# Turning the quantised activations of a two-product FFN by DMA instead of by TensorE

## The chip, the core and the metric

The kernel runs on one core of one Trainium2 chip. Its time is the device time of one launch in microseconds (us). Before the change it is 3245.24 us, the median of three runs (3242.97, 3245.24 and 3245.39).

## What is computed

A gated layer of a Flamingo-like model: cross-attention of 32 batches of 224 tokens (width 512, 16 heads of 32) to 750 context rows of width 384, and then a feed-forward network (FFN) whose two products take quantised activations and quantised weights. Cut to what matters here:

```python
def act_quant(x):                       # per row, to whole numbers of -128..127
    scale = 127.0 / clip(max(abs(x), axis=-1), 1e-5)
    return clip(round(x * scale), -128, 127) / scale
def weight_quant(w):                    # to -1, 0, 1, by the mean of |w|
    ...
def bitlinear(x, w, b):
    return act_quant(rmsnorm(x)) @ weight_quant(w).T + b

x = x + tanh(g_xattn) * cross_attention(layernorm(x), ctx)    # softmax over 750 rows
h = gelu(bitlinear(layernorm(x), w1, b1))                     # 512 -> 2048
x = x + tanh(g_ffn) * bitlinear(h, w2, b2)                    # 2048 -> 512
```

[...] Quantisation works along a row (a token's features), with the token in the partition. So each quantised activation has to be turned, from token x feature to feature x token, before its product can run. How that turning is done is what changes.

## The kernel before

**Two streams of work, woven into one order by hand.** The attention goes through 128 steps: 32 batches, and in each of them four groups of four heads. The loop of line 802 builds one step in six slots. In each slot it first emits a score block on TensorE: in the even slots `maxima` (line 276, tiles `sm`), whose rows VectorE reduces to maxima (`mx`); in the odd slots `weights` (line 333, tiles `se`), whose scores ScalarE exponentiates (`p`) and GpSimd adds up (`acc`). Both use the one PSUM buffer `s` of the pool `ps_s`. So TensorE can't begin a `weights` block before VectorE has read the `maxima` block ahead of it, nor the next `maxima` block before ScalarE has read the `weights` block. What TensorE does in between are the other products of the attention (`pk`, `pv`, `pq`, `po`, `pyt`) and the FFN.

**The FFN** takes 7168 tokens in 28 pairs of 128-row tiles (`ffn_units`, line 507). Per pair: load two tiles of the attention's result back from HBM into `xg` (`a_load`), statistics, centring on ScalarE (`xc`), row maximum, scales, multiplication onto the grid on GpSimd (`a_grid`), rounding to whole numbers in bf16 on ScalarE (`a_round`, tile `xq`, 128 x 1024 for the pair), turning (`a_turn`, line 564, tile `xT`). Then per tile: four products of 128 x 512 (`b_matmul`, `ph`) that VectorE scales into `h`, GELU and square on ScalarE, row maximum, scales, grid on GpSimd (`c_grid`), rounding on ScalarE (`c_round`, tile `hq`, 128 x 2048 bf16), turning in two halves (`c_turn`, line 623, tile `hT`), and two products of 128 x 256 (`c_matmul`, `po<-w2q,hT`), after which VectorE adds into `xg` and the SyncE queue stores the tile (`out`).

A turning by TensorE is one transpose for each 128 x 128 block: 8 for a pair's `xq`, 16 for a tile's `hq`, written to PSUM (`pxq`, `phq`) in bf16. ScalarE copies PSUM to SBUF, one copy of 128 x 1024 for each eight blocks.

**The planner.** `Ffn.fill` (line 727) is called in every slot. It puts in those FFN units that fit into the room left on TensorE, ScalarE and VectorE and that are `ready` (line 698). A unit is a tuple of name, lag, the unit that it follows, its cost on the three engines, and the function: `("turn", 1, "round", 0.6, 1.0, 0, a_turn)` is placed at least one slot after `round` and counts 0.6 us of TensorE and 1.0 us of ScalarE. The lag is counted in slots from the placing of the unit that it follows, not from its end. `before` in `ready` holds back units whose buffer isn't free yet. `xq`, `xT`, `hq` and `hT` have one buffer each (`fp`, `bufs=1`).

**Order on the engines.** Calls through `pe`, `dve`, `act` and `gp` (class `Ordered`, line 43) stay in program order on their engine. Calls of `nc.sync`, which issue all DMAs on the SyncE queue (SP), do not: a scheduler places them. [...] The profile gives nearly every instruction line 51, that of `Ordered`, so tiles tell them apart.

Of the kernel before, what the change touches and what calls it, by code (L numbers as in the profile page):

```python
# [9 lines left out]
BF16 = mybir.dt.bfloat16  # L10
# [14 lines left out]
def flamingo_gated_layer(  # L25
# [15 lines left out]
    nc = tc.nc  # L41
# [9 lines left out]
            return lambda *args, **kw: tc.keep_in_program_order(build(*args, **kw))  # L51

    pe, dve, act = Ordered(nc.tensor), Ordered(nc.vector), Ordered(nc.scalar)
    gp = Ordered(nc.gpsimd)
    P = 128
    B, S, D = x.shape
    CY, M = ctxT.shape[1], ctxT.shape[2]
# [25 lines left out]


    gates = const.tile([P, 2], F32, name="gates")
    nc.sync.dma_start(gates[:, 0:1], g_xattn.partition_broadcast(P))
    nc.sync.dma_start(gates[:, 1:2], g_ffn.partition_broadcast(P))
    tg = const.tile([P, 2], F32, name="tg")
    nc.scalar.activation(tg, gates, AF.Tanh)

    mask_u8 = const.tile([CP, B, NQ], U8, name="mask_u8")
    nc.sync.dma_start(mask_u8, maskT)
    qscale = const.tile([CP, B, NQ], F32, name="qscale")
    nc.vector.tensor_copy(qscale, mask_u8)
    nc.vector.tensor_scalar(qscale, qscale, DH ** -0.5, None, ALU.mult)
# [70 lines left out]

    def load_y(b):
        y_of[b] = yp.tile([P, NYC, M], F32, tag="y", name=f"y_{b}")  # L170
        nc.sync.dma_start(y_of[b], ctxT[b].rearrange("(c p) m -> p c m", p=P))

    def load_x(b):
        x_of[b] = xp.tile([CP, NQ, D], F32, tag="x", name=f"x_{b}")
        nc.sync.dma_start(x_of[b], x[b].rearrange("(t p) d -> p t d", p=CP))


    def q_units(b):
# [213 lines left out]
    def finish(b, g):  # L392

        oT = po_of.pop((b, g))
        pyt = ps_m.tile([P, 2, NQ, P], F32, tag="m", name=f"pyt_{b}_{g}")
        for a in range(2):
            for t in range(NQ):
                at = a * S + t * CP
                pe.transpose(pyt[:CP, a, t, :], oT[:, at : at + CP], ident)
        rd = smp.tile([CP, NQ, HG], F32, tag="rd", name=f"rd_{b}_{g}")  # L400
        dve.reciprocal(
            rd, pyt[:CP, 1].rearrange("p t (j d) -> p t j d", j=HG)[:, :, :, 0]
        )
        yo = smp.tile([CP, NQ, P], F32, tag="yo", name=f"yo_{b}_{g}")
        dve.tensor_tensor(
            yo.rearrange("p t (j d) -> p t j d", j=HG),
            pyt[:CP, 0].rearrange("p t (j d) -> p t j d", j=HG),
            rd.unsqueeze(3).to_broadcast([CP, NQ, HG, DH]),
            ALU.mult,
        )  # L410
        cols = slice(g * P, (g + 1) * P)
        gp.tensor_tensor(x_of[b][:, :, cols], x_of[b][:, :, cols], yo, ALU.add)
        if g == NG - 1:
            nc.sync.dma_start(
                x1_d[b * S : (b + 1) * S, :].rearrange("(t p) d -> p t d", p=CP), x_of[b]
            )


    def weight_units():
# [6 lines left out]
        def fetch(which, i, tag):  # L426
            wl = hp.tile([P, F // 2], F32, tag="h", name=f"{tag}_{which}_{i}")
            if which == 0:
                c, h = divmod(i, NW // NDC)
                n = F * NDC // NW  # L430
                nc.sync.dma_start(wl, w1T[c * P : (c + 1) * P, h * n : (h + 1) * n])
                held[tag, which, i] = wl, w1q[:, c, h * n : (h + 1) * n]
                return
            k = NFC // NW
            nc.sync.dma_start(
                wl.rearrange("p (k d) -> p k d", k=k),
                w2T[i * k * P : (i + 1) * k * P, :].rearrange("(k p) d -> p k d", p=P),
            )
            held[tag, which, i] = wl, w2q[:, i * k : (i + 1) * k, :].rearrange("p k d -> p (k d)")
# [47 lines left out]
    TG = 2  # L487
# [19 lines left out]
    def ffn_units(i):  # L507
# [5 lines left out]

        def a_load():
            s["xg"] = xgp.tile([P, TG, D], F32, tag="xg", name=f"xg_{i}")
            nc.sync.dma_start(s["xg"], x1_d[rows, :].rearrange("(t p) d -> p t d", p=P))

        def a_stats():
            st = smf.tile([P, TG, 6], F32, tag="st2", name=f"st2_{i}")
# [43 lines left out]

        def a_turn():
            s["xT"] = fp.tile([P, TG, NDC, P], BF16, tag="xT", name=f"xT_{i}")
            pt = ps_m.tile([P, TG, NDC, P], BF16, tag="m", name=f"pxq_{i}")
            for t in range(TG):
                for k in range(NDC):
                    pe.transpose(pt[:, t, k, :], s["xq"][:, t, k * P : (k + 1) * P], identb)
            act.copy(s["xT"], pt)  # L570

        def b_matmul(t, f):
            if f == 0:
# [45 lines left out]
        def c_round(t):  # L619
            s["hq", t] = fp.tile([P, F], BF16, tag="hq", name=f"hq_{i}_{t}")  # L620
            act.activation(s["hq", t], s.pop(("h", t)), AF.Identity, bias=magic)

        def c_turn(t, k8):
            if k8 == 0:
                s["hT", t] = fp.tile([P, NFC, P], BF16, tag="hT", name=f"hT_{i}_{t}")
            pt = ps_m.tile([P, 8, P], BF16, tag="m", name=f"phq_{i}_{t}_{k8}")
            for a in range(8):
                k = k8 * 8 + a
                pe.transpose(pt[:, a, :], s["hq", t][:, k * P : (k + 1) * P], identb)
            act.copy(s["hT", t][:, k8 * 8 : k8 * 8 + 8, :], pt)  # L630

        def c_matmul(t, half):
            cols = slice(half * D // 2, (half + 1) * D // 2)
            po = ps_m.tile([P, D // 2], F32, tag="m", name=f"po2_{i}_{t}_{half}")
            for k in range(NFC):
                pe.matmul(
                    po, s["hT", t][:, k, :], w2q[:, k, cols], start=(k == 0), stop=(k == NFC - 1)
                )
            o = s["xg"][:, t, cols]
            dve.scalar_tensor_tensor(o, po, s[f"qb{t}"][1], o, ALU.mult, ALU.add)  # L640
            if half:
                at = (i * TG + t) * P
                nc.sync.dma_start(out[at : at + P, :], s["xg"][:, t, :])

        first = [
            ("load", 0, None, 0, 0, 0, a_load),
# [6 lines left out]
            ("sa2", 1, "sa1", 0, 0, 0, lambda: a_scales(2)),  # L653
            ("grid", 0, "sa2", 0, 0, 0, a_grid),
            ("round", 2, "grid", 0, 1.1, 0, a_round),
            ("turn", 1, "round", 0.6, 1.0, 0, a_turn),
        ]
        parts = [first]
        for t in range(TG):
            part = []  # L660
            for f in range(4):
                part.append((
                    f"b{t}{f}", 0, f"b{t}0" if f else None, 0.9, 0, 0.75,
                    lambda t=t, f=f: b_matmul(t, f),
                ))
            part.append((f"gelu{t}", 1, f"b{t}3", 0, 1.9, 0, lambda t=t: b_gelu(t)))
            part.append((f"square{t}", 1, f"gelu{t}", 0, 1.9, 0, lambda t=t: b_square(t)))
            for a in range(2):
                part.append((f"hm{t}{a}", 1, f"gelu{t}", 0, 0, 1.2, lambda t=t, a=a: b_max(t, a)))
            part.append((f"sb{t}0", 1, f"square{t}", 0, 0, 0.2, lambda t=t: c_scales(t, 0)))  # L670
            part.append((f"sb{t}1", 2, f"sb{t}0", 0, 0, 0.2, lambda t=t: c_scales(t, 1)))
            part.append((f"sb{t}2", 1, f"sb{t}1", 0, 0, 0, lambda t=t: c_scales(t, 2)))
            part.append((f"cgrid{t}", 0, f"sb{t}2", 0, 0, 0, lambda t=t: c_grid(t)))
            part.append((f"cround{t}", 2, f"cgrid{t}", 0, 1.9, 0, lambda t=t: c_round(t)))
            for a in range(2):
                part.append((
                    f"cturn{t}{a}", 0 if a else 2, f"cturn{t}0" if a else f"cround{t}",
                    0.5, 1.0, 0, lambda t=t, a=a: c_turn(t, a),
                ))
            for a in range(2):  # L680
                part.append((
                    f"c{t}{a}", 0 if a else 1, f"c{t}0" if a else f"cturn{t}1",
                    1.8, 0, 0.4, lambda t=t, a=a: c_matmul(t, a),
                ))
            parts.append(part)
        return parts

    class Ffn:
# [9 lines left out]
        def ready(self, pair, unit):  # L698
# [12 lines left out]
            if name[-1].isdigit():  # L711
                t = int(name[len(name.rstrip("0123456789"))])
                (p1, t1), (ph, th) = (divmod(pair * TG + t - n, TG) for n in (1, HB))
                before = {
                    f"b{t}0": [(pair, "turn"), (ph, f"cround{th}"), (p1, f"b{t1}3")],
                    f"square{t}": [(p1, f"square{t1}")],
                    f"sb{t}0": [(pair, f"hm{t}0"), (pair, f"hm{t}1"), (p1, f"sb{t1}2")],
                    f"cround{t}": [(p1, f"cturn{t1}1")],
                    f"cturn{t}0": [(p1, f"c{t1}1")],
                }  # L720
            if name.startswith("square") and any(
                n == "norm" and (p, "round") not in self.at for p, n in self.at
# [44 lines left out]
    w_kv = wkvT.rearrange("(c p) e -> p c e", p=P)  # L767
    load_x(0)
    load_y(0)
    nc.sync.dma_start(wkv_sb[:, :, :D], w_kv[:, :, :D])  # L770
    nc.sync.dma_start(wq_sb, wqT.rearrange("(c p) e -> p c e", p=P))
    nc.sync.dma_start(wkv_sb[:, :, D:], w_kv[:, :, D:])
    load_y(1)
    load_x(1)
    nc.sync.dma_start(b1_sb, b1.partition_broadcast(P))
    nc.sync.dma_start(b2g, b2.partition_broadcast(P))
    norm, turns, qs = q_units(0)
    ks = k_units(0, 0) + k_units(0, 1)
    for unit in norm + ks[:2] + turns + qs[:1]:
# [131 lines left out]
```

## Time and profile before

One execution was profiled. It took 3241.06 us, and its profile spans 3239.3 us of them.

| | busy us | share of the span |
|---|---|---|
| TensorE matmuls (PE) | 3060.1 | 94% |
| TensorE weight loads (PEld) | 1976.6 | 61% |
| VectorE (DVE) | 1712.6 | 53% |
| ScalarE (ACT) | 1647.5 | 51% |
| GpSimd (POOL) | 2069.2 | 64% |
| DMA queue q1, of 16 engines | | 11.0% |

Busy time of TensorE counts a matmul from its start to its modelled end. Matmuls overlap, so the mean duration of a group is longer than what one of them takes from the next. The distance from one start to the next is the better price. The row of a group also tells how long its engine sat idle ahead of it and what ended that idle time ("<-").

### The profile page before, as it was taken

To read this page: it belongs to the slowest core of one execution; us is meant where nothing else is said; L and a number is where in the kernel's file an instruction comes from. 1 tells how busy PE (TensorE), PEld (TensorE's weight loads), DVE (VectorE), ACT (ScalarE), POOL (GpSimd) and SP (SyncE) were. 2 spreads that over 40 slices of the span, in tenths; PEclk is the share of its full clock that TensorE was granted. 3 is DMA by queue.
4 is the path that set the end of the run, shared out by engine and by line. 5 is a ranking of instruction groups with operands and counts; after the bars stand their busy time and mean duration, and the time that the engine had idled before them with its cause. 6 is when DMAs were issued, how large, how long until landed. Compare 5 with 4: busy or idle time off the path is not lost. (4 is left out here: it accounts for less than half of the span.)

```text
span 3239.3 us, 65769 instructions
## 1 busy us (share of the span) xinstructions
PE 3060.1 (94%) x28642; PEld 1976.6 (61%) x28642; DVE 1712.6 (53%) x2501; ACT 1647.5 (51%) x1803; POOL 2069.2 (64%) x3048
## 2 busy tenths in 40 slices
PE   7989999999999999999999999999999999999975
PEld 5655566666666666666666666666666666666643
DVE  4576555554465455555554554555555545545533
ACT  2333555555555455455555554555455455555554
POOL 2565667666666676667666666765676666667664
PEclk9999999999999999999999999999999999999988
DMA  3322111010101001101000111001100011110000
GB/s 134 103 75 65 33 40 40 16 39 26 40 30 36 26 25 33 37 32 40 20 29 30 40 36 39 27 16 40 40 30 26 26 33 37 36 40 20 4 20 29
DMA packets 52817, 120.51 MB, mean 37 GB/s; under 512 B 3888, under 2 KB 3888, under 8 KB 52400
## 3 DMA queue, kind: packets, MB, share of 16 engines
q1 hardware_dynamic: 52528, 116.32, 11.0%
q8 instruction: 223, 3.65, 0.5%
q14 instruction: 66, 0.54, 0.1%
HBM read 86.94 MB, written 29.36 MB: 36 GB/s over the span
## 5 line engine op out<-in xcount | busy, mean ns | idle before, releaser
L51 POOL TENSOR_TENSOR acc<-acc,p 125x896 f32<-125x896 f32 x512 | 1069.4, 2089 | 518.3 <-ACT p L51 497.4
L51 DVE TENSOR_REDUCE mx<-sm 112x4 f32<-112x2000 f32 (+1 forms) x384 | 860.9, 2242 | 986.6 <-PE sm L51 986.6
L51 ACT ACTIVATE p<-se 125x1792 f32<-125x1792 f32 x384 | 638.8, 1664 | 413.1 <-PE se L51 407.1
L51 PE MATMUL pk<-y,wkv_sb 128*128 128x375 f32 x1536 | 537.8, 486 | 15.8 <-DMA wkv_sb<-in_wkvT 12.1
L51 PE MATMUL sm<-kT,qT 32*112 32x500 f32 (+1 forms) x4096 | 426.8, 508 | 35.2 <-ACT p L51 34.7
L51 POOL TENSOR_TENSOR acc<-p 125x896 f32<-125x896 f32 x128 | 267.3, 2089 | 273.0 <-ACT p L51 272.9
L51 ACT COPY kT<-pk 128x375 f32<-128x375 f32 x256 | 120.8, 472 | 581.9 <-PE pk L51 581.3
L51 PEld LDWEIGHTS pk<-y,wkv_sb 128*128 128x128 f32 x1536 | 278.6, 190 | 172.2 <-issue 26.7
L51 PE MATMUL pv_None<-wkv_sb,y 128*125 128x256 f32 x1536 | 364.1, 387 | 0.0
L51 PE MATMUL se<-qT,kT 32*125 32x224 f32 x6144 | 362.7, 349 | 0.0
L51 PE MATMUL po<-p,v 125*32 125x224 f32 x6144 | 321.4, 358 | 0.1
L51 PEld LDWEIGHTS pv_None<-wkv_sb,y 128*125 128x125 f32 x1536 | 278.4, 187 | 69.8 <-issue 33.4
L51 PEld LDWEIGHTS se<-qT,kT 32*125 32x125 f32 x6144 | 297.8, 183 | 0.0
L51 DVE SCALAR_TENSOR_TENSOR h<-ph,qa_am,b_sb 128x512 f32<-128x512 f32 x224 | 163.5, 744 | 197.2 <-PE ph L51 196.1
L51 PEld LDWEIGHTS sm<-kT,qT 32*112 32x112 f32 x4096 | 159.2, 170 | 166.8 <-issue 94.4
L51 PEld LDWEIGHTS po<-p,v 125*32 125x32 f32 x6144 | 188.1, 111 | 115.1 <-issue 40.1
L51 PE MATMUL ph<-w1q,xT 128*128 128x512 fp8e4 x896 | 226.8, 385 | 26.2 <-ACT xT L51 24.0
L51 PE MATMUL po<-w2q,hT 128*128 128x256 fp8e4 x1792 | 221.3, 279 | 13.1 <-DVE xg L51 7.1
L51 PE MATMUL pq<-xnT,wq_sb 128*128 128x224 f32 x1024 | 218.2, 356 | 0.2 <-ACT xnT L51 0.2
L51 PE MATMUL se<-nT,ones 3*125 3x448 bf16 x1536 | 157.2, 396 | 54.2 <-DVE mx L51 45.4
L51 POOL TENSOR_TENSOR x<-x,yo 112x256 f32<-112x256 f32 x128 | 100.6, 786 | 165.3 <-DVE yo L51 135.4
L51 PEld LDWEIGHTS <-hT 128*128 128x128 bf16 x1792 | 174.5, 100 | 48.3 <-issue 17.9
(102 smaller groups left out, 3497.3 us busy)
## 6 DMA issues: line engine op xcount, KB each, us to landing
y<-in_ctxT SPq DMA_DIRECT2D x32, 1125.0 KB, 5.4
x<-in_x SPq DMA_DIRECT2D x32, 448.0 KB, 3.9
x_d<-x SPq DMA_DIRECT2D x32, 448.0 KB, 3.1
xg<-x_d SPq DMA_DIRECT2D x28, 512.0 KB, 3.7
out<-xg SPq DMA_DIRECT2D x56, 256.0 KB, 2.1
wa<-in_w1T SPq DMA_DIRECT2D x8, 512.0 KB, 4.5
wa<-in_w2T SPq DMA_DIRECT2D x8, 512.0 KB, 4.0
wb<-in_w1T SPq DMA_DIRECT2D x8, 512.0 KB, 3.8
```

What stands on the lines that cost most here:

```text
L51: return lambda *args, **kw: tc.keep_in_program_order(build(*args, **kw))
```

## The change

1. `a_turn` no longer issues eight transposes and a copy. It issues two DMA transposes from SBUF to SBUF on the SyncE queue, one for each tile of the pair (128 x 512).
2. `c_turn` no longer comes in two halves of eight transposes and a copy each. It issues one DMA transpose of the whole `hq` (128 x 2048).
3. Both turnings cost the planner nothing on any engine and are placed at once after the rounding (lag 0, before: 1 and 2). The products that read them are placed at least three slots after the turning (before: the first product's `b` in the same slot at the earliest, the second's `c` one slot after the second half).
4. All DMAs now go through `sp = Ordered(nc.sync)`, so the SyncE queue is in program order, transposes and ordinary transfers alike.

```diff
-    gp = Ordered(nc.gpsimd)
+    gp, sp = Ordered(nc.gpsimd), Ordered(nc.sync)
...
         def a_turn():
             s["xT"] = fp.tile([P, TG, NDC, P], BF16, tag="xT", name=f"xT_{i}")
-            pt = ps_m.tile([P, TG, NDC, P], BF16, tag="m", name=f"pxq_{i}")
             for t in range(TG):
-                for k in range(NDC):
-                    pe.transpose(pt[:, t, k, :], s["xq"][:, t, k * P : (k + 1) * P], identb)
-            act.copy(s["xT"], pt)
+                sp.dma_start_transpose(s["xT"][:, t], s["xq"][:, t, :])
...
-        def c_turn(t, k8):
-            if k8 == 0:
-                s["hT", t] = fp.tile([P, NFC, P], BF16, tag="hT", name=f"hT_{i}_{t}")
-            pt = ps_m.tile([P, 8, P], BF16, tag="m", name=f"phq_{i}_{t}_{k8}")
-            for a in range(8):
-                k = k8 * 8 + a
-                pe.transpose(pt[:, a, :], s["hq", t][:, k * P : (k + 1) * P], identb)
-            act.copy(s["hT", t][:, k8 * 8 : k8 * 8 + 8, :], pt)
+        def c_turn(t):
+            s["hT", t] = fp.tile([P, NFC, P], BF16, tag="hT", name=f"hT_{i}_{t}")
+            sp.dma_start_transpose(s["hT", t], s.pop(("hq", t)))
...
-            ("turn", 1, "round", 0.6, 1.0, 0, a_turn),
+            ("turn", 0, "round", 0, 0, 0, a_turn),
...
-                    f"b{t}{f}", 0, f"b{t}0" if f else None, 0.9, 0, 0.75,
+                    f"b{t}{f}", 0 if f else 3, f"b{t}0" if f else "turn", 0.9, 0, 0.75,
...
+            part.append((f"cturn{t}", 0, f"cround{t}", 0, 0, 0, lambda t=t: c_turn(t)))
             for a in range(2):
                 part.append((
-                    f"cturn{t}{a}", 0 if a else 2, f"cturn{t}0" if a else f"cround{t}",
-                    0.5, 1.0, 0, lambda t=t, a=a: c_turn(t, a),
-                ))
-            for a in range(2):
-                part.append((
-                    f"c{t}{a}", 0 if a else 1, f"c{t}0" if a else f"cturn{t}1",
+                    f"c{t}{a}", 0 if a else 3, f"c{t}0" if a else f"cturn{t}",
                     1.8, 0, 0.4, lambda t=t, a=a: c_matmul(t, a),
                 ))
...
-                    f"cround{t}": [(p1, f"cturn{t1}1")],
-                    f"cturn{t}0": [(p1, f"c{t1}1")],
+                    f"cround{t}": [(p1, f"cturn{t1}")],
+                    f"cturn{t}": [(p1, f"c{t1}1")],
```

Everywhere else `nc.sync.dma_start` becomes `sp.dma_start`.

More of the change, by code (lines that the diff above doesn't have):

```diff
@@ L85, in flamingo_gated_layer @@
     gates = const.tile([P, 2], F32, name="gates")
-    nc.sync.dma_start(gates[:, 0:1], g_xattn.partition_broadcast(P))
-    nc.sync.dma_start(gates[:, 1:2], g_ffn.partition_broadcast(P))
+    sp.dma_start(gates[:, 0:1], g_xattn.partition_broadcast(P))
+    sp.dma_start(gates[:, 1:2], g_ffn.partition_broadcast(P))
     tg = const.tile([P, 2], F32, name="tg")
@@ L93, in flamingo_gated_layer @@
     mask_u8 = const.tile([CP, B, NQ], U8, name="mask_u8")
-    nc.sync.dma_start(mask_u8, maskT)
+    sp.dma_start(mask_u8, maskT)
     qscale = const.tile([CP, B, NQ], F32, name="qscale")
@@ L170, in load_y @@
         y_of[b] = yp.tile([P, NYC, M], F32, tag="y", name=f"y_{b}")
-        nc.sync.dma_start(y_of[b], ctxT[b].rearrange("(c p) m -> p c m", p=P))
+        sp.dma_start(y_of[b], ctxT[b].rearrange("(c p) m -> p c m", p=P))
     def load_x(b):
         x_of[b] = xp.tile([CP, NQ, D], F32, tag="x", name=f"x_{b}")
-        nc.sync.dma_start(x_of[b], x[b].rearrange("(t p) d -> p t d", p=CP))
+        sp.dma_start(x_of[b], x[b].rearrange("(t p) d -> p t d", p=CP))
     def q_units(b):
@@ L413, in finish @@
         if g == NG - 1:
-            nc.sync.dma_start(
+            sp.dma_start(
                 x1_d[b * S : (b + 1) * S, :].rearrange("(t p) d -> p t d", p=CP), x_of[b]
@@ L430, in fetch @@
                 n = F * NDC // NW
-                nc.sync.dma_start(wl, w1T[c * P : (c + 1) * P, h * n : (h + 1) * n])
+                sp.dma_start(wl, w1T[c * P : (c + 1) * P, h * n : (h + 1) * n])
                 held[tag, which, i] = wl, w1q[:, c, h * n : (h + 1) * n]
@@ L434, in fetch @@
             k = NFC // NW
-            nc.sync.dma_start(
+            sp.dma_start(
                 wl.rearrange("p (k d) -> p k d", k=k),
@@ L515, in a_load @@
             s["xg"] = xgp.tile([P, TG, D], F32, tag="xg", name=f"xg_{i}")
-            nc.sync.dma_start(s["xg"], x1_d[rows, :].rearrange("(t p) d -> p t d", p=P))
+            sp.dma_start(s["xg"], x1_d[rows, :].rearrange("(t p) d -> p t d", p=P))
         def a_stats():
@@ L642, in c_matmul @@
                 at = (i * TG + t) * P
-                nc.sync.dma_start(out[at : at + P, :], s["xg"][:, t, :])
+                sp.dma_start(out[at : at + P, :], s["xg"][:, t, :])
         first = [
@@ L769, in flamingo_gated_layer @@
     load_y(0)
-    nc.sync.dma_start(wkv_sb[:, :, :D], w_kv[:, :, :D])
-    nc.sync.dma_start(wq_sb, wqT.rearrange("(c p) e -> p c e", p=P))
-    nc.sync.dma_start(wkv_sb[:, :, D:], w_kv[:, :, D:])
+    sp.dma_start(wkv_sb[:, :, :D], w_kv[:, :, :D])
+    sp.dma_start(wq_sb, wqT.rearrange("(c p) e -> p c e", p=P))
+    sp.dma_start(wkv_sb[:, :, D:], w_kv[:, :, D:])
     load_y(1)
     load_x(1)
-    nc.sync.dma_start(b1_sb, b1.partition_broadcast(P))
-    nc.sync.dma_start(b2g, b2.partition_broadcast(P))
+    sp.dma_start(b1_sb, b1.partition_broadcast(P))
+    sp.dma_start(b2g, b2.partition_broadcast(P))
     norm, turns, qs = q_units(0)
```

## The prediction, made before the changed kernel had run

> **What bounds the kernel now.** I read the page first, for the engine that is never free, then the groups by form for the four groups that the change removes, then the waits, then the timeline of a stretch in which tiles are turned.
>
> ```profile
> PE 3060.1 (94%) x28642; PEld 1976.6 (61%) x28642; DVE 1712.6 (53%) x2501; ACT 1647.5 (51%) x1803; POOL 2069.2 (64%) x3048
> ```
>
> TensorE is the bound; the others idle for a third or more. From the groups by form, what goes:
>
> ```profile
> L51 ACT COPY hT<-phq 128x1024 bf16<-128x1024 bf16 x112 | 112.2, 1018 | 58.5 <-PE phq L51 58.4
> ...
> L51 PE MATMUL phq<-identb,hq 128*128 128x128 bf16 x896 | 67.6, 222 | 6.2 <-ACT hq L51 5.9 <-DVE h L51 0.3
> ...
> L51 ACT COPY xT<-pxq 128x1024 bf16<-128x1024 bf16 x28 | 28.3, 1011 | 24.3 <-PE pxq L51 23.6
> ...
> L51 PE MATMUL pxq<-identb,xq 128*128 128x128 bf16 x224 | 18.1, 226 | 21.7 <-ACT xq L51 21.7
> ```
>
> The waits of PE that bear on it (total us, times, longest):
>
> ```profile
> PE se L51 <- DVE mx L51: 45.4, 120, 4.9
> ...
> PE sm L51 <- ACT p L51: 34.7, 52, 1.8
> ...
> PE ph L51 <- ACT xT L51: 24.0, 21, 1.9
> ...
> PE po L51 <- ACT hT L51: 6.0, 5, 3.6
> ```
>
> The first two say that the attention has waits of its own: where too little lies between two score blocks, PE waits for VectorE or ScalarE to empty the one score buffer. The third is a wait that the turning makes: `ph` follows its transposes at once and waits for their copy. The timeline of PE (start, duration):
>
> ```profile
> 1519.31 0.62 PE L51 MATMUL phq<-identb,hq 128*128 128x128 bf16 x8
> 1519.86 1.11 PE L51 MATMUL sm<-kT,qT 32*112 32x250 f32 x16
> 1520.91 0.62 PE L51 MATMUL phq<-identb,hq 128*128 128x128 bf16 x8
> 1521.37 2.11 PE L51 MATMUL pk<-y,wkv_sb 128*128 128x375 f32 x6
> 1523.32 0.55 PE L51 MATMUL pxn<-ident,xn 112*128 112x112 f32 x4
> 1523.80 0.41 PE L51 MATMUL se<-nT,ones 3*125 3x448 bf16 x4
> ```
>
> Eight transposes occupy PE for 0.55 and 0.46 us, start to next start, not 8 x 222 ns. From `sm` to `se` are 3.94 us here, a full stretch.
>
> **What goes from PE.** I summed start-to-start times over the trace: 62.2 us for the 112 blocks of `phq`; 28 x 8 x 0.057 = 12.8 us for `pxq`; and the 24.0 us wait for `xT`. But time freed between score blocks isn't all time won. I cut PE's program order, before and after, at every score block (768 stretches) and priced what lies between at the start-to-start medians of before. In the trace of before a stretch from `sm` to `se` never shrinks below about 3.47 us (rows of 1.9 and of 2.2 us of other work both took 3.47), one from `se` to the next `sm` not below about 2.95; above that it takes its own work plus 1.15 or 1.2 us. The work in the stretches falls by 54.9 us in the new order, the sum with the two floors by 42.6; 12 us go into the attention's own waits. With the 24 us, which that pricing leaves out: **67 us off PE's path**.
>
> **What goes from ScalarE**: 140.5 us of copies, on an engine idle for 49%. I cost it at nothing: the cover is PE's work between score blocks. If copies now stand ahead of an exponential that PE waits for, up to 10 us of the 34.7 come back; this is a bound, not in the sum.
>
> **The end.** The last score block starts at 3145.0; the 94 us behind it are a chain of latencies. The new order leaves four tiles' second products there, not five (31.2 us of PE work, not 40.2), but each turning in the chain costs a transfer in place of 2 to 4 us of transposes and copies. I take 0, bounds -10 and +15.
>
> **What is added: 112 DMA transposes on SP**, two of 128 x 512 per pair and one of 128 x 2048 (512 KB) per tile. None is in the trace. What matters is the landing time L of the large one, from SP's release. The nearest rows, of the DMA issues (KB each, us to landing):
>
> ```profile
> xg<-x_d SPq DMA_DIRECT2D x28, 512.0 KB, 3.7
> out<-xg SPq DMA_DIRECT2D x56, 256.0 KB, 2.1
> ```
>
> As a plain transfer of its size it lands in 3.7 us[...]. [...] The built program gives its tiles as 16 x 128, so 128 of them[...] **5.5 us** (estimate), which I take since it lies by the rows[...]. [...]
>
> **How much cover L has.** In the new program I priced PE's way, with the same floors, from the place where a turning is issued to the first product that reads it: for the 50 tiles ahead of the end, 8.0 or 8.3 us for ten, 10.1 to 11.6 for 34, more for the rest (median 10.3); for pairs 8.0 and up. Of that, the rounding uses a part: in the trace of before `hq` ends 3.7 us (median; 4.7 for many, 6.0 at worst) after PE has reached that place, `xq` 1.0 to 2.8. An example of the median: PE is there at 1502.36, and
>
> ```profile
> 1504.06 1.99 ACT L51 ACTIVATE hq<-h,magic 128x2048 bf16<-128x2048 f32 x1
> ```
>
> ends at 1506.05. So cover for L is 4.3 us for ten tiles and 6.4 or more for the others. Summing what L + 3.7 lacks over the 50 tiles: 0 at L = 3.7, 10 us at 5.5, 33 at 7, 70 at 8, 160 at 10[...]. For pairs nothing up to L = 7, and 2 us at 8. The stalls of before on `hT` (6.0 us) are of this kind.
>
> **The queue.** A transpose waits on SP for the rounding, and `out`, `x_d`, `xg`, `x` and `y` transfers stand behind it. Each is asked for long before its reader; the loads are for two batches ahead. What stands ahead: `out` stores wait for VectorE's last addition, 0.9 us (median) after PE's place and so before `hq`; ten turnings stand behind an `x_d` store that waits for GpSimd's addition, which in before ends 4.8 to 7.6 us after PE's place, but the store comes at least 3.1 us earlier in PE's time, so it is gone by 3.7. Five turnings come 3.6 us after a `y` load (5.4 us to landing) and an `x` load: 1 to 2 us each, within the range. The single buffers cost nothing: the next rounding into `hq` is 17 us away, and PE has done with `hT` before `hq` is rounded.
>
> **Sum**, against the profiled execution's own 3241.06 us (span 3239.3; 4 us under the median of the three runs, which is inside the precision claimed): 3241 - 67 + 10 = **3184 us**.
>
> **Rivals.**
> - *The product waits for its transfer* (slower). One mechanism: the transposes [...]land behind the 6.4 us of cover, and PE, in order, stands at the first `po<-w2q,hT` of each tile. It decides from L = 7.9, where the stalls reach 67 us. At L = 10: 3241 - 67 + 160 + about 10 for the pairs = 3344[...]. For it: three slots are all the cover, of which the rounding takes a third. Against it: both rows of plain transfers, and a queue busy for 11%.
> - *The freed time becomes waits* (no more than the copies' wait is won). `se <- DVE mx` and `sm <- ACT p` already stop PE 172 times. If all of the 42.6 us went there, 3241 - 24 + 10 = 3227. Against it: of the 768 stretches 446 hold more than 2.5 us of other work, above the floor.
> - *No difference*: L at 7.5 to 8.2.
>
> That the change doesn't do what it says is out: the built program holds the 112 transposes and no `phq` or `pxq`.
>
> **Chances.** L below 7.5, with most of the 67 us won: 0.57, between 3155 and 3222. The freed time lost to waits: 0.08, at about 3227. Within 0.2%, about what a measurement of this kernel can tell from no change: 0.05. Slower: 0.30, of which 0.14 up to 3400 and 0.16 beyond. The range from 3155 to 3400 leaves out 0.16 above and some 0.03 below; the likeliest case alone has 3155 to 3222.
>
> **What would show it.** No `phq`, `pxq` and copies; `ph <- ACT xT` gone; `se <- DVE mx` and `sm <- ACT p` up by about 12 us together; a DMA issue row `hT<-hq` near 5.5 us and `xT<-xq` near 3; a new wait of PE `po` on that DMA of about 10 us. I am wrong if that wait is above 67 us, or if the `hT` row is above 8; or if attention stretches don't get shorter though it is short.

## The result, and the profile after

The changed kernel takes 3185.89 us (median of four runs, 3185.74 to 3186.89), the kernel before 3245.31 beside it (3242.97 to 3248.05): a ratio of 0.9818, 95% interval 0.9805 to 0.9831. The profiled execution took 3185.84 us, with a span of 3184.1.

I cut every span at the first and the last score block. "Attention" is what lies between them, "end" what comes after; the start is the rest.

| us of the profiled span | start | attention | end |
|---|---|---|---|
| before | 20.9 | 3124.1 | 94.3 |
| after | 22.3 | 3052.5 | 109.2 |
| difference | +1.4 | -71.6 | +14.9 |

The attention, as a window of before and then of after (start and end, length, busy time and instructions of PE, PEld, DVE, ACT and POOL, granted clock, share of the DMA engines, GB/s):

```profile
20.88:3145.02 3124.14, 2998.27 (x28216) 1937.32 (x28216) 1677.94 (x2436) 1599.02 (x1758) 2019.21 (x2903) 1.00 0.11 36
22.32:3074.84 3052.52, 2943.71 (x27223) 1888.55 (x27223) 1672.54 (x2440) 1481.25 (x1633) 2027.74 (x2917) 0.99 0.17 48
```

PE is busy 54.6 us less there, and length less busy time, its idle time, is 17.1 us less (125.9 to 108.8). e7, e8 and e9 below place the attention's work as after does and take 3054.7 to 3054.9, so differences of some 2 us between attentions mean nothing.

The first line of the page of after answers to that of before: PE's work fell by 64 us and the span by 55, so its share of the span stayed at 94%.

```profile
PE 2996.3 (94%) x27522; PEld 1920.3 (60%) x27522; DVE 1705.7 (54%) x2501; ACT 1515.2 (48%) x1663; POOL 2069.3 (65%) x3048
```

`phq`, `pxq` and their copies are gone, and so is the wait `ph <- ACT xT`. The products that read the turned tiles, with the features in the partitions, are as many as before (1792 of `po<-w2q,hT 128*128 128x256`, 896 of `ph<-w1q,xT 128*128 128x512`). The waits of PE (total us, times, longest):

```profile
PE se L51 <- DVE mx L51: 60.7, 153, 4.8
PE po L51 <- DMA hT<-hq: 60.1, 5, 25.0
PE sm L51 <- ACT p L51: 29.6, 40, 1.9
```

The attention's own waits, first and third row, are up by 15.3 and down by 5.1: together 10 us of the freed time ended there. The second row is the new wait. It looks like the forecast's failure, until it is asked for by stage. The same view of PE, from 3074 us to the end only:

```profile
PE po L51 <- DMA hT<-hq: 58.9, 4, 25.0
```

All but 1.2 us of the wait lie in the end, where PE has nothing left to do between a tile's steps. The DMA issues (KB each or none, median us from issue to landing) show why the attention has almost none:

```profile
xg<-x_d SPq DMA_DIRECT2D x28, 512.0 KB, 3.6
out<-xg SPq DMA_DIRECT2D x56, 256.0 KB, 2.0
...
xT<-xq SPq DMA_TRANSPOSE x56, 2.5
hT<-hq SPq DMA_TRANSPOSE x56, 4.3
```

The large transpose lands in 4.3 us, not 5.5. SP's own part of that is in the views of the two tiles (ns min, median and max of the issue, first and last start); first `hT`, 128 tiles of 16 x 128 per transpose in the built program:

```profile
L51 SPq DMA_TRANSPOSE hT<-hq x56: 1317/1819/3081, 435.7 to 3170.3; - x56
...
DMA to landing us min/median/max: 4.2/4.3/6.0
```

then `xT`, 32 tiles:

```profile
L51 SPq DMA_TRANSPOSE xT<-xq x56: 1189/1260/2456, 348.0 to 3127.2; - x56
...
DMA to landing us min/median/max: 2.4/2.5/4.4
```

96 tiles more cost the queue 0.56 us, which is 5.8 ns each, and the landing 1.8 us, 18.8 ns each.

### The profile page after: what moved, and what is told of

Same layout as the page of the kernel before. It is cut to its first block, busy times and chain, and to the rows that moved or that the text cites. A ratio compares the mean times of both kernels' runs of the same rounds, so it can differ in the third digit from the quotient of the medians.

```text
span 3184.1 us, 63629 instructions
## 1 busy us (share of the span) xinstructions
PE 2996.3 (94%) x27522; PEld 1920.3 (60%) x27522; DVE 1705.7 (54%) x2501; ACT 1515.2 (48%) x1663; POOL 2069.3 (65%) x3048
## 3 DMA queue, kind: packets, MB, share of 16 engines
q1 hardware_dynamic: 199472, 153.03, 17.4%
## 4 chain that ended last, share of the span: by engine, by line
PE 77%; DVE 14%; ACT 4%; POOL 3%; issue 1%; DMA 1%; SPq 0%; ACTq 0%; POOLq 0%; DVEq 0%
PE po L51 16%; PE se L51 13%; PE sm L51 12%; DVE mx L51 11%; PE pk L51 10%; PE pv_None L51 9%; PE ph L51 6%; PE pq L51 4%; PE pv L51 4%; ACT p L51 2%; ACT L51 1%; POOL acc L51 1%; PE pyt L51 1%; DVE xn L51 1%; PE pxn L51 1%
## 5 line engine op out<-in xcount | busy, mean ns | idle before, releaser
L51 PE MATMUL sm<-kT,qT 32*112 32x500 f32 (+1 forms) x4096 | 426.7, 508 | 30.2 <-ACT p L51 29.6
L51 PE MATMUL se<-nT,ones 3*125 3x448 bf16 x1536 | 157.4, 396 | 64.6 <-DVE mx L51 60.7
```

## The experiments

"Attention" and "end" are cut as above; each run's ratio is to runs of the kernel before on the same chip.

| run | us (median) | ratio (95%) | attention | end |
|---|---|---|---|---|
| e1_order | 3243.5 | 1.000 (0.9991 to 1.0009) | 3125.4 | 94.0 |
| e2_wait | 3255.8 | 1.004 (1.0025 to 1.0055) | 3119.7 | 114.7 |
| e3_second_only | 3199.0 | 0.9862 (0.9848 to 0.9877) | 3064.7 | 109.7 |
| e4_first_only | 3239.7 | 0.9987 (0.9978 to 0.9995) | 3106.6 | 110.9 |
| e5_twice | 3314.8 | 1.0204 (1.0187 to 1.0221) | 3165.5 | 126.4 |
| e6_lag2 | 3213.1 | 0.9896 (0.9882 to 0.9911) | 3079.3 | 112.8 |
| e7_end_by_pe | 3171.5 | 0.9763 (0.9748 to 0.9777) | 3054.9 | 93.8 |
| e8_end_short_lags | 3190.4 | 0.983 (0.9814 to 0.9847) | 3054.7 | 112.6 |
| e9_end_pe_lag3 | 3171.9 | 0.9773 (0.9759 to 0.9788) | 3054.8 | 94.6 |
| e10_quarters | 3192.2 | 0.9835 (0.982 to 0.9849) | 3057.4 | 110.7 |

### The ordered queue alone (e1)

The kernel before, with the fourth part of the change only:

```diff
-    gp = Ordered(nc.gpsimd)
+    gp, sp = Ordered(nc.gpsimd), Ordered(nc.sync)
```

and `sp.dma_start` for every `nc.sync.dma_start`.

> The kernel before with one edit: all DMAs in program order on the SyncE queue; transposes stay on TensorE. My theory (the order costs and gains nothing in the attention, where SP waits for work anyway): 3241 us, within 5. Rival (a part of the gain is the loads' new order): more than 10 us faster than before.

3243.5 us against 3244.1: nothing. The waits of PE are those of before to a tenth of a microsecond or three. The start is 1.3 us longer here, but it varies by as much between runs with this same order of the queue (20.9 us in e3, 21.0 in e8, 22.4 in e5), so the +1.4 of after need not come from the change.

### The placement wait alone (e2)

TensorE still turns, but the product that stood at once behind its transposes is placed a slot later:

```diff
-                    f"b{t}{f}", 0, f"b{t}0" if f else None, 0.9, 0, 0.75,
+                    f"b{t}{f}", 0 if f else 1, f"b{t}0" if f else "turn", 0.9, 0, 0.75,
```

> The kernel before with one edit: the first product of a pair is placed at least one slot after its turning by TensorE, so that it no longer follows its transposes at once. My theory: the 24 us wait of `ph` for the copy `xT` is a matter of placing and goes without any DMA; three us more come out of the stretches, one tile more in the end takes back some: 3220 us, within 8. Rival (the wait is only moved, as the time goes into the attention's own waits): 3235 or more.

A clear miss: not 20 us faster, but 12 slower. The waits of PE:

```profile
PE phq L51 <- ACT hq L51: 40.6, 4, 20.5
...
PE ph L51 <- ACT xT L51: 2.5, 1, 2.5
```

The wait did go, from 24.0 to 2.5 us (last line), and of the 21.0 us that it took in the attention nothing is left there. But the attention became only 4.4 us shorter, and the end 20.4 longer. In the end the trace holds 192 matmuls `po<-w2q,hT`, six tiles' second products where before had 160, and the first line is a wait of that chain. One lag more had moved a tile's work behind the last score block. In the attention PE's idle time fell by 10.0 us, but its busy time grew by 5.6, with the granted clock at half for 22 us more (last section).

The largest losses are in single stretches between two score blocks, which take 4 to 6 us above their price (the priced rule of the prediction). Between 300 and 3050 us before has two (5.2 and 5.0), e2 four (6.4, 5.9, 5.9 and 4.4), after one of 3.9. This is one of before (start, duration, and in brackets the idle time ahead with its releaser):

```profile
1505.00 4.29 POOL L51 TENSOR_TENSOR acc<-acc,p 125x896 f32<-125x896 f32 x2
1505.08 4.50 DVE L51 TENSOR_SCALAR xn<-x,mv,ve 112x512 f32<-112x512 f32 x2 [3.23 <-POOL ve L51]
...
1509.50 0.47 DVE L51 SCALAR_TENSOR_TENSOR xg<-po,qb_am,xg 128x256 f32<-128x256 f32 x1
...
1510.02 3.41 PE L51 MATMUL po<-w2q,hT 128*128 128x256 fp8e4 x16 [3.57 <-DVE xg L51]
```

VectorE stands 3.23 us at `xn` until GpSimd's `ve` is there; the addition into `xg`, behind it in VectorE's order, starts at 1509.50 only, so the PSUM buffer isn't read, and PE waits 3.57 us for that. Most of PE's wait is not VectorE's standing, which is over at 1505.08, but the length of the two `xn`: 4.50 us together. In the tile's view (ns min, median and max) one of them takes 0.95 us in the median:

```profile
L51 DVE TENSOR_SCALAR xn<-x,mv,ve x64: 534/952/2987, 13.1 to 2975.9; 112x512 f32<-112x512 f32 x64
```

The 24 of the 64 that have GpSimd's `acc` beside them for over three quarters of their time, as here, take 2.28 us in the median (0.54 to 2.99; 13 take more than 2.2), the other 40 take 0.54 (1.41 at most). That the two slow each other down is inferred from this; no run tests it.

One of e2's four is of the same kind. In two others it is ScalarE that stands, at a rounding that waits for GpSimd's `h` (8.92 us in the one below), with the copy `v` behind it that PE needs and waits 5.50 us for:

```profile
1618.35 2.00 ACT L51 ACTIVATE hq<-h,magic 128x2048 bf16<-128x2048 f32 x1 [8.92 <-POOL h L51]
1620.26 0.56 ACT L51 COPY v<-pv_None 125x512 f32<-125x512 f32 x1
...
1620.87 1.01 PE L51 MATMUL pxn<-ident,xn 112*128 112x112 f32 x4 [5.50 <-ACT v L51]
```

The fourth, and the one of after, is a wait for VectorE's `h`. That they come and go with the placing is read from the traces; no run tested it alone. What follows: the 24 us were a wait that could be removed, but not a gain by themselves. Removing it needs a plan that has a place for the work.

### One product each (e3, e4)

e3 turns only `hq` by DMA; `a_turn` and the first product's placing are those of before:

```diff
-            ("turn", 0, "round", 0, 0, 0, a_turn),
+            ("turn", 1, "round", 0.6, 1.0, 0, a_turn),
```

> Of the changed kernel, only the second product's activations (`hq`, 112 of the blocks of eight) are turned by DMA; the pair's `xq` stays on TensorE with its copy, and its product follows at once. My theory: the stretches between score blocks lose 33 us by the pricing of before, the wait for `xT` stays, the end gets 15 us longer: 3223 us, within 8. Rival (the freed time becomes waits): 3235 or more.

e4 turns only `xq` by DMA; `c_turn` in two halves with its units and lags is that of before.

> Of the changed kernel, only the first product's activations (`xq`) are turned by DMA, with the product three slots later; `hq` stays on TensorE. My theory: 24 us of wait and 11 us of the stretches go, one tile more in the end takes some back: 3210 us, within 8. Rival (a transfer in place of the copy only moves the wait): `ph` waits for the DMA of `xT`, and the time is 3230 or more.

The larger share went to the other part than expected: attention -59.5 for the second product alone, -17.5 for the first. Together 77, where the change as a whole has 71.6, so they nearly add up there; both pay the end (+15.4 and +16.6). In e3 the wait for `xT` halved although nothing of the first product was touched:

```profile
PE ph L51 <- ACT xT L51: 11.0, 10, 1.1
```

and none of the long stretches is left between 300 and 3050 us. In e4 three of them are 4.5 us or more above their price, and its residual above the prices is 60.4 us, hardly under the 66.9 of before (after: 37.8). So what is called the price of a wait here depends on where the plan puts everything else.

### A landing twice as long (e5)

The same transpose is issued two times, with the same data:

```diff
-            sp.dma_start_transpose(s["hT", t], s.pop(("hq", t)))
+            for _ in range(2):
+                sp.dma_start_transpose(s["hT", t], s["hq", t])
```

> The changed kernel, but each `hq` is turned twice into the same tile, the second DMA after the first has landed, so that the landing time seen by the product is about 8.6 us in place of 4.3. My theory (cover decides): with the distances that the trace of after shows between landing and first product (0.3 to 7.7 us, median 2.4), 4.3 us more cost 77 us of stalls in the attention and some 15 in the end: 3278 us, within 15, slower than the kernel before. PE's `po` waits for the DMA `hT` for over 120 us. Rival (the landing is off the path, the gain is all TensorE's work): below 3215.

One transpose lands after 4.3 us here too (median), and the queue waits for the first to land before it issues the second (56 waits, 141.2 us), so a pair lands after 8.6 us. PE's waits, over the span and then in the attention only:

```profile
PE po L51 <- DMA hT<-hq: 162.3, 45, 29.3
```

```profile
PE po L51 <- DMA hT<-hq: 86.3, 41, 6.0
```

From 5 waits for the transpose to 45. One of them, in PE's timeline:

```profile
1517.36 1.92 PE L51 MATMUL po<-w2q,hT 128*128 128x256 fp8e4 x16 [2.02 <-DMA hT<-hq]
```

and the queue ahead of it, in SP's (the transposes were issued from 1508.52):

```profile
1508.52 6.35 SPq L51 DMA_TRANSPOSE hT<-hq  x2
1514.97 3.03 SPq L51 DMA_TRANSPOSE xT<-xq  x2
```

1508.52 + 8.6 is 1517.1, and PE begins at 1517.36. The attention is 113 us longer than after's, and the kernel 2% slower than before: this is the first rival, made real by 4.3 us more of landing. The mechanism is confirmed, and 111 of the 113 lie in stretches that hold a second product. 77 us of stalls were expected; the waits for the transpose in the attention are up by 85, from 1.2 to 86.3 us, and PE's idle time there by 84. What was left out of the forecast is the clock: the same matmuls keep PE busy for 29 us longer (2972.8 for 2943.7), with the granted clock at half for 92 us of the attention, in after for 38. The 54.6 us more at half clock explain 27 of the 29 at most.

### One slot less (e6)

The second product at two slots behind its turning:

```diff
-                    f"c{t}{a}", 0 if a else 3, f"c{t}0" if a else f"cturn{t}",
+                    f"c{t}{a}", 0 if a else 2, f"c{t}0" if a else f"cturn{t}",
```

> The changed kernel with the second product placed at least two slots after its turning, not three. My theory: 15 or so of the 50 tiles then have a distance of 5.0 to 5.9 us from issue to product, in which the rounding (3.3) and the landing (4.3) don't fit; 34 us of stalls: 3218 us, within 12. Rival (three slots are more than needed): 3190 or less.

PE's waits in the attention:

```profile
PE se L51 <- DVE mx L51: 64.5, 163, 4.9
PE sm L51 <- ACT p L51: 35.9, 48, 1.9
PE po L51 <- DMA hT<-hq: 18.6, 15, 5.5
```

Attention +27 against 34 expected, but the stalls at the transpose are up by 17 only, half of what was expected. The attention's own waits are up by 10 (first two lines; 60.7 and 29.6 in after), smaller waits down by 8, and PE's busy time is 7 longer, with 10 us more at half clock. With e5 it brackets the cover from both sides: take a slot from it, or add a landing to what it must hide, and the stalls come.

### The end (e7, e8, e9)

The end costs 15 us more than before. Is that the transfers' latency, or the lag of three slots that the new plan asks for? Three kernels change only the last two pairs. e7 turns them by TensorE with the units, lags and costs of before:

```diff
+    LAST = 2
...
-            ("turn", 0, "round", 0, 0, 0, a_turn),
+            ("turn", 0, "round", 0, 0, 0, a_turn) if i < NF - LAST else ("turn", 1, "round", 0.6, 1.0, 0, a_turn),
```

(and so for `c_turn`, `b` and `c`).

> The changed kernel, but the last two of the 28 pairs are turned by TensorE as before (units, lags and costs of before for them); the 26 pairs beside the attention stay with DMA. My theory: the attention part is as short as in the changed kernel (3052 us from first to last score block), and the end takes 94 us or a little less, not 109: 3170 us, within 5. Rival (the end is longer for another reason than the transfers, such as the new lags of the tiles ahead of it): 3180 or more.

e8 keeps the DMA transposes and shortens the lags of the last two pairs to those of before (0 for `b`, 1 for `c`):

> The changed kernel, but for the last two pairs the products may follow their turnings as closely as in the kernel before (lag 0 for `b`, 1 for `c`); all turnings stay DMA transposes. It tells apart what made the end shorter when TensorE turned the last two pairs. My theory (the transfers' latency in the chain of the end): no change, the end stays at 109 us, 3185 us within 5. Rival (the lags of three slots): the end falls to about 94 us, 3170 us.

e9 is e7 with the lags of three:

> The last two pairs are turned by TensorE, as in the run that did this before, but with lags of three slots for their products, as in the changed kernel. My theory (latency of transfers, not lags): the end is 94 us or less, 3171 us or less; it may gain a few us, since the first product of the last pair then stands ahead of a second product of the pair before it and fills a wait. Rival (the lags): 3185 us.

The end is 93.8 us in e7, 94.6 in e9 and 112.6 in e8. TensorE or DMA decides it, the lags don't. e7, at 3171.5 us, is faster than both kernels: its interval of ratios (0.9748 to 0.9777) lies clear of after's. The few microseconds that I hoped for from e9 did not come. How the latency comes about, in the timeline of after's end:

```profile
3110.44 2.00 ACT L51 ACTIVATE hq<-h,magic 128x2048 bf16<-128x2048 f32 x1 [9.83 <-POOL h L51]
3112.47 1.89 SPq L51 DMA_TRANSPOSE hT<-hq  x1
...
3116.82 5.55 PE L51 MATMUL po<-w2q,hT 128*128 128x256 fp8e4 x32 [25.00 <-DMA hT<-hq]
3116.88 2.00 ACT L51 ACTIVATE hq<-h,magic 128x2048 bf16<-128x2048 f32 x1 [4.44 <-DMA hT<-hq]
...
3122.93 0.34 SPq L51 DMA_DIRECT2D out<-xg  x1
3123.37 1.89 SPq L51 DMA_TRANSPOSE hT<-hq  x1
3125.37 3.07 SPq L51 DMA_TRANSPOSE xT<-xq  x2
3127.87 5.16 PE L51 MATMUL po<-w2q,hT 128*128 128x256 fp8e4 x32 [5.50 <-DMA hT<-hq]
```

The first rounding ends at 3112.44, SP starts 0.03 us later, and PE begins when the transpose has landed at 3116.8. Then a second cost: the next rounding (3116.88) had to wait for the single `hq`, which the transpose reads until it lands, and its own transpose started at 3123.37, 4.5 us after it (in the last pair 5.4). Of these, 3.5 us are the single `hT`, which the product ahead reads until 3122.37; the rest is the `out` store, which stands ahead in the queue and waits for VectorE's last addition. The same place in e7, by TensorE:

```profile
3112.75 1.89 PE L51 MATMUL phq<-identb,hq 128*128 128x128 bf16 x16 [22.74 <-ACT hq L51]
3114.89 5.41 PE L51 MATMUL po<-w2q,hT 128*128 128x256 fp8e4 x32 [0.25 <-ACT hT L51]
3120.13 1.06 PE L51 MATMUL phq<-identb,hq 128*128 128x128 bf16 x16
3121.90 3.71 PE L51 MATMUL po<-w2q,hT 128*128 128x256 fp8e4 x32 [0.71 <-ACT hT L51]
```

There the first rounding ends at 3112.69, so from it to its product's start are 2.2 us, not 4.4, and the second tile's product follows 7.0 us behind the first's, not 11.0: `hq` comes free with the last transpose (the next rounding starts at 3115.63), and TensorE writes the next one to PSUM from 3120.13, before the product that reads `hT` ends at 3120.30. In the last pair the same two differences are 2.1 and 4.5 us. The four add up to 12.8 of the 15.4 us between the two ends.

### The transpose in quarters (e10)

```diff
-            sp.dma_start_transpose(s["hT", t], s.pop(("hq", t)))
+            for k in range(0, NFC, 4):
+                sp.dma_start_transpose(
+                    s["hT", t][:, k : k + 4, :], s["hq", t][:, k * P : (k + 4) * P]
+                )
```

> The changed kernel, but each `hq` is turned by four DMA transposes of 128 x 512 in place of one of 128 x 2048; the first product reads all four. By the issue rows of after (a transpose of 128 x 512 keeps SP for 1.26 us and lands 2.5 us after its start) the last one lands after 3 x 1.26 + 2.5 = 6.3 us, not 4.3. My theory (each instruction has its own cost on SP, and cover decides): 2 us more cost 7 us in the attention and 8 in the end: 3200 us, within 6. Rival (the cost goes by bytes alone, so four quarters land as early as one whole): 3186 us, within 3.

The queue's view of the tile:

```profile
L51 SPq DMA_TRANSPOSE hT<-hq x224: 1188/1260/2551, 434.9 to 3180.5; - x112
```

Four issues of 1.26 us in place of one of 1.82: the last quarter lands 6.4 us after the first issue (6.3 expected), so one large transpose lands earlier than four. The time does not show it clearly: the interval of ratios overlaps that of after. The +4.9 us in the attention and +1.5 in the end are under the 7 and 8 expected, and PE's idle time in the attention did not grow (107.6 us, in after 108.8; the waits for the transpose are 3.1 of it). What grew is its busy time, by 6 us with 10 us more at half clock, and half of that is there in e8 too, which places the attention as after does. PE begins the product up to 2.2 us before the last landing beside the attention and 3.9 in the end, so its first matmuls wait for their quarter only, not for all four.

## Why the prediction was right, and where its terms were off

The sum gave 3184 against 3185.84 of the profiled execution. The mechanism held; that the number did is partly luck, for terms off by about 9 and 6 us one way and 15 the other cancelled.

- **What goes from PE's path** (67): 71.6. The work held: PE's busy time in the attention fell by 54.6 us, where 54.9 were summed. 10 us of the freed time went into `se <- DVE mx` and `sm <- ACT p`, where 12 were expected, so the rival of the freed time becoming waits held to that share and no further. The wait for `xT` gave 21.0 us there, as the other 3 of the 24 lay in the end. The remaining 6 are smaller waits that went, above all the 7.1 us at `xg` in the two long stretches of before, which the pricing could not see. (In the prices, the sum falls by 42.6 us and what lies above them by 29, from 66.9 to 37.8.)
- **The landing time L** (5.5): 4.3. The 5.5 was my estimate, and not shown: the trace of before holds no DMA transpose. It was too high. SP was busy for 1.8 us with the large one and 1.26 with the small, which makes 5.8 ns per tile and a fixed 1.1 us (estimate from these two medians); the landing came 2.5 us after the 1.8. The second small one of a pair lands 1.26 + 2.5 = 3.8 us after the first is issued (estimate from its two medians). The plain transfer of the same size comes nearest: 4.3 against the 3.6 us of `xg`, 512 KB.
- **The cover**: PE's way from the turning to its product was priced at 8.0 us at least, median 10.3; measured 8.1 and 10.2. The rounding ends 3.7 us into it, as in before. From landing to product 0.3 to 7.7 us are left (median 2.4), and the stalls in the attention are 1.2 us, where 10 were in the sum, a consequence of L. e5 and e6 show that the cover is what decides. The break-even of L = 7.9 lies between the two points measured: at 4.3 the attention is 72 us shorter than before, at 8.6 it is 41 longer, where the prediction's own stalls (70 us at 8, 160 at 10) would give some 30. Of the 6.0 us on `hT` in before, which the prediction set beside these stalls, 5.7 lie in the end.
- **The end** (0, bounds -10 and +15): +14.9, at the bound. The failed step is that four tiles in place of five would balance the transfers. The new order did leave one tile less, 9 us of products and transposes, and PE's busy time there fell by 10.6 us (53.7 to 43.1). But its time without work grew by 25.5: each turning costs a landing, and two of them stood for 4.5 and 5.4 us more, for `hT` and the `out` store. "The single buffers cost nothing" held in the attention, where the next use is far away, and failed here. e7, e8 and e9 show that it is the transfers; by the timelines of after and e7 the later first products are 4.3 us of it and the later second ones, where buffers and store come in, 8.5. No run gives `hq` or `hT` a second buffer, or moves the store out of the way, so that split is a reading and not an experiment.
- **ScalarE at nothing**: `sm <- ACT p` fell, so no part of the 10 us bound came, and none of it came back either.
- **The queue** (1 to 2 us, within the range): nothing in the attention, as e1 has it. The loads `x` and `y` do land later, `x` after 6.9 us instead of 3.9 and `y` after 6.3 instead of 5.4, but most of that is the program order (6.7 and 5.9 in e1, without a transpose), and no wait of PE for them appears. `xg` (3.6, before 3.7) and `out` (2.0, before 2.1) weren't slowed.

Open: how far a placement can be told ahead. e2, e3 and e4 were each missed by 24 to 36 us, though the sum of the whole change held. The planner's response, with its 5 us stretches and its end, is a size that I had no price for, and so is the clock after a stall.

## What to carry to other kernels

In this kernel, where TensorE is the bound, a transpose by DMA was nearly free where the plan left more than its landing between the last producer and the first reader; work that out as distance on PE, less the producer's delay, and price the landing by the transfer of its size, which here was right within 0.6 us (3.7 in the trace of before, 4.3 measured). In a chain with no other work, the end above all, the same landing is bare (the end takes 109.2 us in after, 93.8 in e7): turn by TensorE there, and look for single buffers and for an in-order queue whose store stands ahead. A wait removed by moving a unit in a planned order is worth only what the new plan makes of it: e2 removed 21 us of it and lost 12.

## What the runs showed that I had not expected

A short gap on PE can be paid twice. After gaps of 1.9 to 3.9 us in these traces the granted clock falls to half for 3.4 us, at times for 6.8 (10.2 once, at 3045.6 us of after), though not after each (none follows the 2.96 us at 436 us of after): in e5, between 300 and 3050 us, after 7 of the 8 gaps above 2.5 us and 5 of the 18 between 1.8 and 2.5. Half clock begins there 1.7 to 4.6 us after the gap has begun. Around the stretch of before shown above, by windows as above:

```profile
1500.00:1506.00 6.00, 6.00 (x47) 4.09 (x45) 2.54 (x10) 3.50 (x3) 4.76 (x17) 1.00 0.00 0
1506.00:1510.00 4.00, 0.45 (x6) 0.16 (x3) 4.00 (x4) 0.84 (x3) 3.92 (x3) 1.00 0.00 0
1510.00:1513.40 3.40, 3.38 (x17) 2.55 (x17) 3.40 (x3) 0.00 (x0) 3.32 (x3) 0.53 0.44 135
```

PE is idle in the second window and at clock 0.53 in the third: the 16 matmuls of `po` take 3.41 us there, against 1.92 in the stretch of e5 shown above, after a gap of 2.02 us that left the clock alone. So this stall of 3.57 us on PE's path cost about 5 (estimate: 3.57, and the 1.49 by which the 16 matmuls took longer), of which the wait shows only the 3.57. A shorter gap was enough elsewhere: 2.26 us at 718 us of after, followed by 3.4 at half.

The transposes also filled the queue with small packets: q1's share of the DMA engines' time went from 11.0 to 17.4%, for 37 MB more (256-byte packets of 18 ns, the median), without a wait that could be seen.
